# Three placements in the second layer of a two-layer network: convolution pieces, a pair of scalings, and the silu of the third u

## The chip, the cores and the metric

The kernel runs on one core of a Trainium2 chip. The metric is the device time of one execution in microseconds (us), the median of several runs. A profile is one further execution, recorded instruction by instruction. Its engines are PE (matrix multiply; PEld is its weight load), DVE (vector), ACT (scalar, activation functions), POOL (GpSimd) and SP, which here only issues DMAs.

## The reference

The input x has shape 4 x 192 x 128 x 128 in float32. Layer 1 adds a block of fractional and ordinary Fourier transforms; nothing in it is touched here. Layer 2 adds a selective state-space block to x, along the 16384 pixels of an image taken as one sequence:

```python
seq = (seq - mu) * lax.rsqrt(var + LN_EPS) * ln_g + ln_b
xz = jnp.einsum('blc,ec->ble', seq, in_proj_w)
xs, z = jnp.split(xz, 2, axis=-1)
# xc: a causal convolution of 4 taps over xs, channel by channel, + conv_b
u = jax.nn.silu(xc).transpose(0, 2, 1)
x_dbl = jnp.einsum('bld,kd->blk', u, x_proj_w)
dt, Bm, Cm = jnp.split(x_dbl, [DT_RANK, DT_RANK + D_STATE], axis=-1)
dt = jax.nn.softplus(jnp.einsum('blr,dr->bld', dt, dt_proj_w) + dt_proj_b)
A = -jnp.exp(A_log)
def step(hcar, inp):
    dt_t, B_t, C_t, u_t = inp
    dA = jnp.exp(dt_t[..., None] * A)
    hnew = hcar * dA + (dt_t * u_t)[..., None] * B_t[:, None, :]
    y_t = jnp.sum(hnew * C_t[:, None, :], axis=-1)
    return (hnew, y_t)
...
y = ys.transpose(1, 0, 2) + u * Dp
y = y * jax.nn.silu(z)
out = jnp.einsum('bld,cd->blc', y, out_proj_w)
```

There are 384 inner channels and 16 states for each.

## The kernel before

The sequence of each image is cut into 32 chunks of T = 512 pixels, 128 chunks for the four images. The 384 channels are NJ = 3 groups of 128 (one per partition). A chunk is worked in 24 *steps*, k = 0 to 23: group j = k // 8 and pair of states sg = k % 8. A step holds two *scans*, one for each state of the pair. Scan k.0 and scan k.5 are the first and the second of step k.

What a step does, engine by engine:

- DVE runs the two scans (L869), h = h * da + db. The factor `da` = exp(dt * A) comes from ACT (L799). For most scans it lies in a tile `da`, prepared four scans ahead, and the other operand is a PSUM tile `op`.
- The second operand is made in one of three ways. In the steps where sg is 3 or 6 (`BY_PE`), ACT scales blocks of the transposed dt*u by B (`scale_pair`, L843, tile `dbT`, from a transposed copy `tu` that PE writes at L833), and PE transposes them back (`turned_back`, L855, into `op`). In the steps 1, 4, 7, 9, 15, 17 and 23 (`BY_POOL`) POOL multiplies (L827, tile `db`), two steps ahead. There the factor of the scan stands in a PSUM `op`, made by ACT three scans ahead (`decay_there`). In all others DVE multiplies (L819), from dp, an ACT copy of dt*u in PSUM (L782).
- POOL multiplies the two states with C (L882, `hc` <- `h`). The tile h has three buffers, hc five.
- PE sums hc into y by transposing it (L895), three steps later.

Next to these steps runs the *front* of a later chunk, a Python generator, `front(i)`: normalisation, projections, convolution, the making of u, z, dt and B, C. It begins at step 14 of the chunk two before its own, runs through all of the chunk before its own, and each plain `yield` ends its part in one step. `yield MID` puts the next part between the two scans of the same step, `yield LATE` behind both scans. The order of the instructions on each engine is the order in which the Python code emits them (`manual_schedule`). In a step, the emission goes: tails of an earlier chunk, the first `turned_back`, sums, `turned`, the fronts' first parts, POOL's db for the step after next, then the first scan; after it the second `turned_back`, the MID parts and the scalings (`between`); then the second scan, POOL's hc, and the LATE parts.

The front's parts that matter here, with their steps in the chunk before its own: projections of xs (`in_proj`, L666) in step 23 of the chunk before that and in steps 0 and 1 and their copies by ACT (L679) in 0, 1 and 2; the convolution on PE, four taps for each group, in halves (`conv`, L684): c0 in steps 2 and 3, c1 in 4 and 6, c2 in 9 and 10; silu of the first two u in step 8 (L692); projection of z0 in step 12; silu of the third u and of z0 (L692, L696) at the head of step 13; the projection of B, C and dt (px, L728) in step 14.

The front of the chunk after that is at its normalisation in steps 14 to 22: sums on PE (L619, step 15), the centring on DVE (L622, step 16), the variance (L635, step 18), the root on ACT (`rs`, L642, behind step 19's scans), its reciprocal on DVE (L645) and the transpose on PE (L647) behind step 20's scans, the copy `rows` on ACT (L651) and its spreading on PE (L655) in step 21, and the multiplication on DVE (L660) between the scans of step 22.

`TURNED` and `SCALED` say in which steps PE turns a group and ACT scales its pairs. Each group's y is copied by ACT (L904), transposed by PE (L919) and gated by DVE (L924) once a chunk, in the next group's steps. PSUM for the fronts' and tails' products and for `tu` is one pool of three buffers (`ps`). SP issues the DMAs of the carried states and of B and C.

Of the kernel before, what the change touches and what calls it, by code (L numbers as in the profile page):

```python
# [503 lines left out]
def layer1(tc, xmid, out, st2, w, n_tok=S * S):  # L504
# [10 lines left out]
    MID, LATE = "mid", "late"  # L515

    TURNED = {0: 0, 9: 1, 15: 2, 19: 2}
    SCALED = {0: (0, 3), 3: (0, 6), 9: (1, 3), 11: (1, 6), 16: (2, 3), 19: (2, 6)}
    with ExitStack() as ctx:
        def pool(name, bufs, **kw):  # L520
            return ctx.enter_context(tc.tile_pool(name=name, bufs=bufs, **kw))
# [66 lines left out]
        def psum():  # L588
            return ps1.tile([128, 512], F32, name="ps")
# [14 lines left out]
        def front(i):  # L604
# [58 lines left out]
            def in_proj(m):  # L663
                pp = psum()
                for t in range(2):
                    nc.tensor.matmul(  # L666
                        pp, wiT[:, t, m * 128 : (m + 1) * 128], s[:, t, :], start=t == 0, stop=t == 1
                    )
                return pp
# [6 lines left out]
            for j in range(NJ):  # L676
                pp = in_proj(j)
                yield
                nc.scalar.activation(xs[:, j, 3:], pp, AF.Identity, bias=bxz[:, j : j + 1])  # L679
            nc.scalar.copy(halo, xs[:, :, T : T + 3])  # L680

            def conv(j, pc, half):
                for k in (2 * half, 2 * half + 1):
                    nc.tensor.matmul(  # L684
                        pc, dcw[:, j, k, :], xs[:, j, k : k + T], start=k == 0, stop=k == 3
                    )
# [3 lines left out]
            def silu_u(j, pc):  # L690
                u[j] = jp.tile([128, T], F32, name="u")
                nc.scalar.activation(u[j], pc, AF.Silu, bias=cb[:, j : j + 1])  # L692

            def silu_z(j, pp):
                zs[j] = jp.tile([128, T], F32, name="zs")
                nc.scalar.activation(zs[j], pp, AF.Silu, bias=bxz[:, NJ + j : NJ + j + 1])  # L696
# [18 lines left out]
            c2 = psum()  # L715
            conv(2, c2, 0)
            yield
            conv(2, c2, 1)
            yield
            yield  # L720
            z0 = in_proj(NJ)
            yield
            silu_u(2, c2)
            silu_z(0, z0)
            yield
            px = psum()
            for j in range(NJ):
# [109 lines left out]
        def scale_pair(n, j, sg):  # L837

            g = got[n]
            for st in range(sg * G, (sg + 1) * G):  # L840
                t = g["dbT", j, st] = scp.tile([128, T // 128, 128], F32, name="dbT", bufs=2)
                for blk in range(T // 128):
                    nc.scalar.activation(  # L843
                        t[:, blk, :], g["tu", j][:, blk, :], AF.Identity,
                        scale=g["bT"][:, blk, st : st + 1],
                    )
# [102 lines left out]
        def start_front(n):  # L949
            if n < total:  # L950
                fronts.append(front(n))
# [10 lines left out]
        def go_on(parts, part):  # L962

            for f in parts[part]:
                got_on = next(f, None)
                if got_on is not None:
                    parts[got_on].append(f)

        with tc.manual_schedule():
            for i in range(min(2, total)):  # L970
                load_x(i)
            for _ in front(0):
                pass
# [18 lines left out]
            for pos, (n, k) in enumerate(order):  # L992
# [26 lines left out]
                def between():  # L1019
                    go_on(parts, MID)  # L1020
                    if k in SCALED and k:
                        scale_pair(n, *SCALED[k])

# [4 lines left out]
                if k == 0:  # L1028
                    scale_pair(n, *SCALED[k])
                if pos >= LAG and sg == LAG:  # L1030
# [130 lines left out]
def program(tc, x, out, w):  # L1161
    B = x.shape[0]
    with (
        tc.tile_pool(name="keep", bufs=1) as keep,
        tc.tile_pool(name="mid", bufs=1, space=DRAM) as mid,
    ):
        st2 = keep.tile([CH, B, 2, 2], F32, name="st2")
        xmid = [mid.tile([C, S * S], F32, name=f"xmid{b}") for b in range(B)]
        layer0(tc, x, xmid, st2, w)
        layer1(tc, xmid, [out[b].rearrange("c h w -> c (h w)") for b in range(B)], st2, w)  # L1170
# [16 lines left out]
```

## Time and profile before

| | |
|---|---|
| time, median of 3 runs (lowest, highest) | 11583.59 us (11582.08, 11585.74) |
| the profiled execution: its time | 11592.76 us |
| the profiled execution: its span | 11590.8 us |
| mean granted TensorE clock | 0.934 |
| between 2500 and 11000 us (layer 2): POOL, DVE, PE, ACT busy | 8225.6, 8158.0, 8056.5, 7596.2 of 8500 us |
| scan (L869), one | 1267 ns |
| hc on POOL (L882), one | 2366 ns |

The span runs from the first to the last recorded instruction; layer 1 takes about the first 1500 us. In the lists a line gives the source line, the engine, the operation and the tiles as out<-in. In the timeline the first two numbers are the start and the length in us, and the brackets at the end hold the idle time of the engine before it and what ended it. In the list of waits a line says who waited for whom: us in total, times, longest. "issue" stands where the profile shows no releaser.

### The profile page before, as it was taken

The page shows a single profiled execution, that of the slowest core. Times are in us where ns is not written, and L with a number is a line of the kernel's source. Part 1 is how long each engine was busy: PE and PEld are TensorE (multiplying, and loading weights), DVE is VectorE, ACT ScalarE, POOL GpSimd, SP SyncE. Part 2 cuts the span into 40 slices and gives each one's busy share as a digit, 9 for nine tenths or more (in the row PEclk, how much of TensorE's full clock was granted, in tenths as well). Part 3 has the DMA queues.
Part 4 walks back from the last instruction along what each step waited for, and adds up shares of the span by engine and source line. Part 5 has one row for each costly group of instructions (what it writes and reads, how often), then busy time and mean ns, then how long its engine had stood idle before and what let it go on. Part 6 is the DMA issues. An engine that isn't in the chain of part 4 may idle for free.

```text
span 11590.8 us, 163663 instructions
## 1 busy us (share of the span) xinstructions
PE 10615.0 (92%) x54154; PEld 7007.7 (60%) x54154; DVE 10503.1 (91%) x11072; ACT 9334.7 (81%) x17508; POOL 9823.7 (85%) x4470
## 2 busy tenths in 40 slices
PE   4777889999999999999999999999999999999998
PEld 2444356666666666666666666666666666666665
DVE  5565679999999999999999999999999999999999
ACT  2322178988988988988898898898898889889887
POOL 0000069999999999999999999999999999999999
PEclk8878789999999999999999999999999999999999
DMA  8787734434434434433433443443443443444343
GB/s 206 204 218 203 195 102 126 114 115 126 121 108 127 127 103 126 126 108 121 126 113 116 126 120 109 127 126 103 127 126 107 122 126 112 117 126 118 111 126 98
DMA packets 1339433, 1494.73 MB, mean 129 GB/s; under 512 B 903474, under 2 KB 954359, under 8 KB 1338071
## 3 DMA queue, kind: packets, MB, share of 16 engines
q1 hardware_dynamic: 1318102, 1421.34, 42.8%
q0 software_dynamic: 13312, 50.34, 1.3%
q10 hardware_dynamic: 7168, 12.59, 0.3%
q8 instruction: 428, 7.01, 0.3%
q14 instruction: 423, 3.46, 0.1%
HBM read 1325.19 MB, written 155.32 MB: 128 GB/s over the span
## 4 chain that ended last, share of the span: by engine, by line
PE 35%; DVE 28%; ACT 23%; issue 11%; DMA 2%; POOL 1%; DVEq 0%; SPq 0%; ACTq 0%; POOLq 0%
DVE h L869 18%; PE ps L666 8%; ACT da L799 7%; PE py L895 7%; PE ps L684 6%; DVE op L819 5%; PE ps L933 3%; ACT dbT L843 3%; ACT L799 3%; PE op L855 3%; ACT op L799 2%; PE pr L471 2%; ACT s L612 2%; ACT L692 1%; ACT L642 1%
## 5 line engine op out<-in xcount | busy, mean ns | idle before, releaser
L882 POOL TENSOR_TENSOR hc<-h,bc 128x1024 f32<-128x1024 f32 x3072 | 7195.0, 2366 | 342.6 <-DVE h L869 338.2
L869 DVE TENSOR_TENSOR_SCAN h<-da,carry,op 128x512 f32<-128x512 f32 x4216 | 5227.0, 1267 | 115.2 <-PE op L855 110.9
L895 PEld LDWEIGHTS py<-ident,hc 128*128 128x128 f32 x24576 | 2963.8, 147 | 787.8 <-issue 716.3
L895 PE MATMUL py<-ident,hc 128*128 128x128 f32 x24576 | 3360.5, 283 | 25.7 <-POOL hc L882 12.4
L799 ACT ACTIVATE da<-dt,c_A_log 128x512 f32<-128x512 f32 x4352 | 3008.5, 728 | 356.9 <-DVE h L869 349.4
L869 DVE TENSOR_TENSOR_SCAN h<-op,carry,db 128x512 f32<-128x512 f32 x1736 | 2203.2, 1269 | 116.7 <-issue 83.6
L827 POOL TENSOR_TENSOR db<-dtu,bc 128x1024 f32<-128x1024 f32 x896 | 2146.2, 2395 | 6.4 <-DMA bc<-dbc 6.4
L819 DVE TENSOR_TENSOR op<-dp,bc 128x512 f32<-128x512 f32 x2816 | 1897.8, 674 | 32.1 <-ACT dp L782 32.1
L843 ACT ACTIVATE dbT<-ps,bT 128x128 f32<-128x128 f32 x6144 | 1656.8, 379 | 11.8 <-PE ps L833 11.6
L799 ACT ACTIVATE op<-dt,c_A_log 128x512 f32<-128x512 f32 x1792 | 1222.3, 683 | 548.0 <-DVE h L869 546.5
L666 PE MATMUL ps<-s,c_wiT 96*128 96x512 f32 x3072 | 1602.6, 648 | 2.6 <-DVE s L660 2.6
L684 PE MATMUL ps<-xs,dcw 128*128 128x512 f32 x3072 | 1448.4, 594 | 4.2 <-ACT xs L679 1.8
L855 PE MATMUL op<-ident,dbT 128*128 128x128 f32 x6144 | 1084.1, 297 | 102.2 <-DVE h L869 78.3
L855 PEld LDWEIGHTS op<-ident,dbT 128*128 128x128 f32 x6144 | 795.1, 152 | 528.5 <-ACT dbT L843 149.1
L799 ACT ACT_TABLE_LOAD x636 | 816.0, 1283 | 11.2
L666 PEld LDWEIGHTS ps<-s,c_wiT 96*128 96x128 f32 x3072 | 556.7, 201 | 420.4 <-issue 417.1
L933 PE MATMUL ps<-yg,c_woT 128*96 128x512 f32 x1536 | 710.4, 598 | 57.0 <-DVE xm L939 57.0
L684 PEld LDWEIGHTS ps<-xs,dcw 128*128 128x128 f32 x3072 | 523.4, 190 | 380.4 <-issue 371.6
L477 POOL DMA_DIRECT2D xmid<-xt x64 | 42.6, 666 | 792.3 <-DVE xt L475 792.3
L742 PE MATMUL ps<-xd,c_dtT 12*128 12x512 f32 x768 | 443.6, 662 | 99.4 <-ACT dbT L843 76.0
L751 POOL TENSOR_TENSOR dtu<-dt,u 128x512 f32<-128x512 f32 x384 | 477.8, 1272 | 29.5 <-ACT dt L747 29.5
L933 PEld LDWEIGHTS ps<-yg,c_woT 128*96 128x96 f32 x1536 | 239.8, 163 | 423.7 <-issue 307.7
(172 smaller groups left out, 10399.8 us busy)
## 6 DMA issues: line engine op xcount, KB each, us to landing
bc<-dbc SPq DMA_DIRECT2D x1024, 1024.0 KB, 5.8
xt<-in_x SPq DMA_DIRECT2D x192, 768.0 KB, 9.2
xmid<-xt POOLq DMA_DIRECT2D x64, 768.0 KB, 7.1
xm<-xmid SPq DMA_DIRECT2D x128, 384.0 KB, 3.8
carry<-h SPq DMA_DIRECT2D x3072, 1.0 KB, 1.9
out<-xm SPq DMA_DIRECT2D x128, 384.0 KB, 3.3
d<-x ACTq DMA_DIRECT2D x64, 192.0 KB, 8.2
df<-u SPq DMA_DIRECT2D x16, 512.0 KB, 5.0
```

The costliest lines, as they stand in the source:

```text
L666: nc.tensor.matmul(pp, wiT[:, t, m * 128 : (m + 1) * 128], s[:, t, :], start=t == 0, stop=t == 1)
L684: nc.tensor.matmul(pc, dcw[:, j, k, :], xs[:, j, k : k + T], start=k == 0, stop=k == 3)
L751: nc.gpsimd.tensor_tensor(dtu[j], dt[j], u[j], ALU.mult)
L799: nc.scalar.activation(da, got[n]["dt"][j], AF.Exp, scale=A[:, j, st : st + 1])
L819: nc.vector.tensor_tensor(dbs[s], g["dp"], g["bc", k % NG][:, 0, q, :], ALU.mult)
L827: nc.gpsimd.tensor_tensor(db, _bc(g["dtu"][j], 1, G), g["bc", sg][:, 0], ALU.mult)
L843: nc.scalar.activation(t[:, blk, :], g["tu", j][:, blk, :], AF.Identity, scale=g["bT"][:, blk, st : st + 1],)
L855: nc.tensor.transpose(db[:, blk * 128 : (blk + 1) * 128], t[:, blk, :], ident)
L869: nc.vector.tensor_tensor_scan(h[:, q, :], das.pop(s), dbs.pop(s) if db is None else db[:, q, :], 0.0 if ch == 0 else g["before"][:, j, st ...
L882: nc.gpsimd.tensor_tensor(hc, h, g["bc", sg][:, 1], ALU.mult)
L895: nc.tensor.matmul(py[:, blk, :], hc[:, q, blk * 128 : (blk + 1) * 128], ident, start=first, stop=sg == NG - 1 and q == G - 1 and blk == T ...
L933: nc.tensor.matmul(po[0:CH], woT[:, j, t * CH : (t + 1) * CH], g["yg", j], start=j == 0, stop=j == NJ - 1,)
```

## The change

Nothing is added or taken out; five placements differ. The line numbers after the second hunk are larger by 1 to 3 in the changed file.

```diff
@@
-    SCALED = {0: (0, 3), 3: (0, 6), 9: (1, 3), 11: (1, 6), 16: (2, 3), 19: (2, 6)}
+    SCALED = {0: (0, 3), 3: (0, 6), 9: (1, 3), 11: (1, 6), 16: (2, 3), 20: (2, 6)}
@@
                 yield
                 nc.scalar.activation(xs[:, j, 3:], pp, AF.Identity, bias=bxz[:, j : j + 1])
             nc.scalar.copy(halo, xs[:, :, T : T + 3])
+            yield LATE
 
             def conv(j, pc, half):
@@
             c2 = psum()
             conv(2, c2, 0)
             yield
+            yield LATE
             conv(2, c2, 1)
             yield
-            yield
             z0 = in_proj(NJ)
             yield
+            yield MID
             silu_u(2, c2)
             silu_z(0, z0)
+            yield
             yield
             px = psum()
```

In steps: the first half of c0 moves from the head of step 2 to behind its scans, and so on PE from before to behind the second `turned_back` of that step. The second half of c2 moves in the same way in step 10. The projection of z0 moves from the head of step 12 to the head of step 11. The silu of the third u and of z0 move from the head of step 13 to between the scans of step 12. The scalings of pair (2, 6) move from between the scans of step 19, ahead of the root, to between those of step 20, behind it. All that follows (px and on) stays in its step.

## What was predicted

> **What bounds the kernel now.** I read the page, then the waits and busy times of one long stretch of layer 2, then the timelines of POOL, DVE, ACT and PE through one chunk.
>
> ```profile
> PE 10615.0 (92%) x54154; PEld 7007.7 (60%) x54154; DVE 10503.1 (91%) x11072; ACT 9334.7 (81%) x17508; POOL 9823.7 (85%) x4470
> ...
> POOL hc L882 <- DVE h L869: 271.2, 428, 1.4
> ...
> DVE rs L645 <- ACT rs L642: 120.2, 108, 2.1
> ...
> DVE h L869 <- PE op L855: 95.3, 181, 1.3
> ...
> DVE h L869 <- issue: 74.7, 109, 1.0
> ```
>
> The first line is the page's busy line, the others are the waits between 2500 and 11000 us. There layer 2 runs at 78.50 us a chunk (first scan to first scan), so the stretch holds 108.3 chunks. In its 8500 us the windows view gives POOL 8225.6 busy and DVE 8158.0: both nearly full, with 2.53 and 3.16 us idle a chunk. No edit shortens work of either, so the most there is to win is POOL's idle time, 2.53 x 127 chunks = 321 us. I number steps 0 to 23 in a chunk, two scans each (k.0, k.5). POOL's timeline through one chunk (first scan at 6241.6 us) shows where it is idle:
>
> ```profile
> 6266.26 2.41 POOL L827 TENSOR_TENSOR db<-dtu,bc 128x1024 f32<-128x1024 f32 x1
> 6268.62 9.32 POOL L882 TENSOR_TENSOR hc<-h,bc 128x1024 f32<-128x1024 f32 x4
> 6278.69 2.38 POOL L882 TENSOR_TENSOR hc<-h,bc 128x1024 f32<-128x1024 f32 x1 [0.75 <-DVE h L869]
> 6282.26 2.37 POOL L882 TENSOR_TENSOR hc<-h,bc 128x1024 f32<-128x1024 f32 x1 [1.19 <-DVE h L869]
> ...
> 6298.87 2.35 POOL L882 TENSOR_TENSOR hc<-h,bc 128x1024 f32<-128x1024 f32 x1 [0.30 <-DVE h L869]
> ...
> 6316.76 2.35 POOL L882 TENSOR_TENSOR hc<-h,bc 128x1024 f32<-128x1024 f32 x1 [0.20 <-DVE h L869]
> ```
>
> Four waits, each for DVE: hc of steps 11, 12, 17 and 22. By place over 108 chunks they average 0.69, 1.20, 0.30 and 0.34. From hc(22) on POOL has no gap until hc(11) of the next chunk. DVE's own stalls in the same chunk:
>
> ```profile
> 6251.95 1.28 DVE L869 TENSOR_TENSOR_SCAN h<-da,carry,op 128x512 f32<-128x512 f32 x1 [0.84 <-PE op L855]
> ...
> 6268.71 1.28 DVE L869 TENSOR_TENSOR_SCAN h<-op,carry,db 128x512 f32<-128x512 f32 x1 [0.16 <-POOL db L827]
> ...
> 6277.27 1.28 DVE L869 TENSOR_TENSOR_SCAN h<-da,carry,op 128x512 f32<-128x512 f32 x1 [0.21 <-PE op L855]
> ...
> 6288.64 1.28 DVE L869 TENSOR_TENSOR_SCAN h<-op,carry,db 128x512 f32<-128x512 f32 x1 [0.67 <-issue]
> ...
> 6309.69 0.18 DVE L645 RECIPROCAL rs<-rs 128x4 f32<-128x4 f32 x1 [0.98 <-ACT rs L642]
> ...
> 6314.18 1.22 DVE L660 TENSOR_TENSOR s<-s,ps 96x1024 f32<-96x1024 f32 x1 [0.16 <-PE ps L655]
> ```
>
> These are scans 3.5, 9.0, 11.5, 15.0, the reciprocal at the end of step 20, and the multiply inside step 22 (means 0.73, 0.21, 0.17, 0.69, 1.10, 0.17). The two lists make one ring. From hc(22) to db(9) POOL leads: scan 9.0 waits for db(9) in every chunk, so a DVE stall before it (3.5) costs nothing. From 9.0 to 12.5 DVE leads, and POOL's waits at 11 and 12 are the other face of that run. From hc(12) to hc(22) POOL leads again, but for the late scans at 17 and 22.
>
> ACT tells why 15.0 is late; "issue" names nothing, but the scan begins 0.09 after the first op below is done (6287.88 + 0.67 = 6288.55):
>
> ```profile
> 6282.12 0.72 ACT L799 ACTIVATE da<-dt,c_A_log 128x512 f32<-128x512 f32 x1 [1.05 <-DVE h L869]
> 6282.77 0.59 ACT L782 COPY dp<-dtu 128x512 f32<-128x512 f32 x1
> 6283.37 1.28 ACT L692 ACT_TABLE_LOAD   x1
> ...
> 6287.88 0.67 ACT L799 ACTIVATE op<-dt,c_A_log 128x512 f32<-128x512 f32 x1
> ```
>
> ACT idles 0.47 + 1.05 us before two da, then two table loads and two silu hold up everything, and it does not idle again until 6316.6.
>
> [...] op(3.5) stands behind 1.72 us of convolution (6249.53 to 6251.25). [...] The trace has the 1.28, but silu follows 0.02 later, so I take 1.28 alone. In the changed program's order the scalings after the root bring no load, and all 1311 loads of the program remain. [...]
>
> **The change part by part** (times of this chunk; no instruction is added or removed, DVE's, POOL's and SP's orders stay).
>
> 1. *First convolution pieces behind op(3.5)*, step 2. op(3.5) comes up to 1.72 us earlier, which covers the 0.73. DVE reaches 7.0 and 9.0 that much earlier and waits there for db(7) and db(9). Worth 0. Displaced: conv, then py; hc has five buffers and no row shows POOL waiting for PE here.
>
> 2. *Second half of c2 behind op(11.5)*, step 10. Without the 1.72, op(11.5) can be done near 6275.6; scan 11.5 wants it at 6277.06. DVE leads here: -0.17.
>
> 3. *z0's projection a step earlier, silu in the middle of step 12.* PE: conv until about 6277.3, z0 until 6279.1; silu's first load can start at 6279.88, when ACT has finished the two da before. The 3.88 us block (6283.37 to 6287.25) then fills the 1.52 idle. Queued behind it: da(14.0), ready at 6279.88 + 3.88 + 0.72 = 6284.48; scan 14.0 wants it at 6285.52 - 0.21 = 6285.31, a margin of 0.83. Then da(14.5), dp, da(16.0), and op(15.0) ready about 6287.0, wanted at 6287.75 when scan 14.5 ends. So 15.0's 0.69 goes, and DVE is 0.17 + 0.69 = 0.86 earlier at step 17, POOL by 0.17: hc(17) no longer waits: -0.30. ACT does not keep its 1.55: op(17.5) needs the slot that scan 16.0 frees, and before it started 0.04 after that scan's end (6293.46, 6293.50), so ACT runs 0.86 earlier from there on.
>
> 4. *Pair (2,6) scaled behind the root*, step 20. Eight scalings take 2.00 us (6304.60 to 6306.60), so the root is done at 6309.66 - 2.00 - 0.86 = 6306.8; DVE wants it near 6307.9. The 1.10 at the reciprocal vanishes. Next is late: rows (L651), behind the same ACT work as before (2.00 only changed place), so it moves by 0.86 alone: 6312.73 to 6311.87. PE's L655 and the multiply inside step 22 follow; their wait grows from 0.17 to about 1.2. DVE is 0.86 earlier at 22.5, POOL by 0.47: hc(22)'s wait of 0.34 goes, with 0.05 left over. New waits: the pair's scalings (ready about 6308.9, wanted as op(22.0) at 6310.9), and the transpose of rs, whose PSUM buffer is now the one these scalings read: ready at 6308.9, PE comes to it behind the yt transposes at about 6309. If this cover were gone, op(22.0) and rows would be late by what the scalings are, and past 0.05 us it would cost part of the 0.34.
>
> Sum: -0.17 - 0.30 - 0.34 = -0.81 a chunk, times 127 = -102 us. POOL's waits at 11 and 12 stay, at 1.72 together. Against the profiled execution (span 11590.8, its time 11592.76) that is 11490.5; the median shown is 9.2 lower, 11583.6, so the forecast is 11482.
>
> Bounds of what before does not show: part 3's margin of 0.83 may prove too small (a loss below), or POOL may gain less than 0.81 if ACT's lead fades before rows. At most all idle but 11 and 12 goes, 0.17 + 0.64, which is the forecast itself; small shifts in semaphore lag (0.09 a hand-over, some two in the DVE-led run) give 0.2 x 127 = 25 us either way.
>
> **Rivals.**
> - *Only part of it* (18%): the lead at rows is 0.47 or less, since a da or op waits for a DVE event that I took as free. hc(22) keeps its wait: 0.47 x 127 = 60, 11524. For: one gate had 0.04 of margin. Against: the others I followed have 0.3 or more.
> - *Every DVE stall counts* (5%): 0.73 + 0.17 + 0.69 + 1.10 = 2.69, capped by POOL's 2.53, times 127 = 321: 11262. For: DVE is the busier-looking engine of the waits view, and POOL's 271 all name it. Against: scan 9.0 waits for POOL in all chunks, so what DVE gains before it ends there.
> - *No change* (6%): op(15.0) is not what 15.0 waits for, and the root's 2.00 is paid back at rows: only 0.17 x 127 = 22, 11562.
> - *Slower* (6%): the silu block delays da(14.0). It decides from 0.83 + 0.86 = 1.7 us of delay (silu of z would begin at 6281.8, so z0 would have to end 4.4 us after its 6279.1); below that POOL at hc(17) is no later than before. At 2.5 us of delay, 0.8 a chunk: 11583.6 + 102 = 11686. PE without a gap here speaks for it; ACT getting to z 2.7 us after z0 is done against.
>
> **How the numbers follow.** The walk as a whole: 65%, 11482, by itself 11457 to 11507. The part case adds its 11524 with as much above, so the range is 11450 to 11535; it leaves out no change, slower and most of the third rival. Below 0.2% (23 us) this kernel can't be told from no change. Faster: 65 + 18 + 5 = 88%; same 6%; slower 6%.
>
> **What would show it.** Right: no wait at 3.5, 11.5, 15.0 and the reciprocal; about 1 us at 7.0 and 9.0 for POOL, and about 1.2 at L660 for PE; POOL with two waits a chunk, 77.7 us a chunk. Wrong: POOL still waiting at hc(17) or hc(22), or DVE waiting for da at 14.0.

## The result, and the profile after

| | before | after |
|---|---|---|
| time, median of 4 runs (lowest, highest) | 11583.12 us (11582.08, 11585.74) | 11453.55 us (11448.41, 11459.74) |
| profiled execution: time, span | 11592.76, 11590.8 us | 11449.58, 11447.4 us |
| first to last scan of layer 2 | 10044.9 us | 9915.1 us |
| period of a chunk in layer 2 | 78.50 us | 77.49 us |
| mean granted TensorE clock | 0.934 | 0.931 |

The changed kernel takes 0.9888 of the time of before, 95% interval 0.9871 to 0.9905: 129.6 us less. Layer 2 accounts for it: from its first to its last scan it takes 129.8 us less, 1.01 us a chunk. (Between the two profiled executions layer 1 differs by another 13.6 us; nothing in it was edited, and the medians don't show that.)

The busy line of the page, after:

```profile
PE 10543.1 (92%) x54154; PEld 7050.4 (62%) x54154; DVE 10489.8 (92%) x11072; ACT 9324.7 (81%) x17508; POOL 9806.5 (86%) x4470
```

POOL and DVE lost 17 and 13 us of busy time against a span shorter by 143: it was idle time that went. The waits of the changed kernel between 2500 and 11000 us (total, times, longest):

```profile
POOL hc L885 <- PE ps L922: 125.3, 105, 1.2
...
DVE s L660 <- PE ps L655: 122.0, 110, 1.2
...
DVE h L872 <- POOL db L830: 101.6, 292, 0.7
...
POOL hc L885 <- DVE h L872: 50.5, 113, 1.2
...
DVE h L872 <- ACT da L802: 7.9, 25, 0.5
```

DVE no longer waits for `op` or for the root; it waits for POOL (`db`), at the multiply of step 22 for PE, and a little for `da` at scan 22.0. The first line is to be read with care. It is the wait of hc(12), and the releaser named is not what ends it. In POOL's timeline of the chunk that begins at 6165.9 us:

```profile
6192.94 9.34 POOL L885 TENSOR_TENSOR hc<-h,bc 128x1024 f32<-128x1024 f32 x4
6202.72 2.38 POOL L885 TENSOR_TENSOR hc<-h,bc 128x1024 f32<-128x1024 f32 x1 [0.44 <-DVE h L872]
6206.29 2.36 POOL L885 TENSOR_TENSOR hc<-h,bc 128x1024 f32<-128x1024 f32 x1 [1.19 <-PE ps L922]
...
6217.94 6.98 POOL L885 TENSOR_TENSOR hc<-h,bc 128x1024 f32<-128x1024 f32 x3
...
6237.85 4.87 POOL L885 TENSOR_TENSOR hc<-h,bc 128x1024 f32<-128x1024 f32 x2
```

hc(12) starts at 6206.29, and scan 12.5, whose output it reads, ends at 6206.11: POOL waits for DVE there as before (over 107 chunks hc(12) starts 0.17 us after that scan's end, in both kernels). The lines with x3 and x2 hold hc(17) and hc(22), now without a gap before them. DVE in the same chunk (scans 4.0, 7.0, 9.0, the reciprocal, scan 22.0, the multiply):

```profile
6176.73 1.28 DVE L872 TENSOR_TENSOR_SCAN h<-op,carry,db 128x512 f32<-128x512 f32 x1 [0.17 <-POOL db L830]
...
6186.07 1.28 DVE L872 TENSOR_TENSOR_SCAN h<-op,carry,db 128x512 f32<-128x512 f32 x1 [0.40 <-POOL db L830]
...
6193.05 1.28 DVE L872 TENSOR_TENSOR_SCAN h<-op,carry,db 128x512 f32<-128x512 f32 x1 [0.39 <-POOL db L830]
...
6232.02 0.17 DVE L645 RECIPROCAL rs<-rs 128x4 f32<-128x4 f32 x1
...
6235.40 1.28 DVE L872 TENSOR_TENSOR_SCAN h<-da,carry,op 128x512 f32<-128x512 f32 x1 [0.28 <-ACT da L802]
...
6237.79 1.22 DVE L660 TENSOR_TENSOR s<-s,ps 96x1024 f32<-96x1024 f32 x1 [1.12 <-PE ps L655]
```

And ACT around the silu, whose two loads stood behind 0.47 + 1.05 us of idle time before and now follow the da without a gap:

```profile
6202.84 1.39 ACT L802 ACTIVATE da<-dt,c_A_log 128x512 f32<-128x512 f32 x2
6204.24 1.28 ACT L693 ACT_TABLE_LOAD   x1
...
6206.82 1.28 ACT L802 ACT_TABLE_LOAD   x1
...
6210.49 0.67 ACT L802 ACTIVATE op<-dt,c_A_log 128x512 f32<-128x512 f32 x1
```

The op of scan 15.0 is done at 6211.16 and DVE starts that scan at 6211.93 without a wait. By place, in us a chunk over 108 chunks:

| idle time | before | after |
|---|---|---|
| DVE at 3.5, 4.0, 7.0, 9.0 | 0.73, 0, 0.06, 0.21 | 0, 0.19, 0.38, 0.38 |
| DVE at 11.5, 15.0, reciprocal | 0.17, 0.69, 1.10 | 0, 0, 0 |
| DVE at 22.0 and the multiply (L660) | 0, 0.17 | 0.13, 1.11 |
| POOL at hc(11), hc(12), hc(17), hc(22) | 0.69, 1.20, 0.30, 0.34 | 0.42, 1.19, 0, 0.03 |

### The profile page after: what moved, and what is told of

The parts are those of the page before. It is cut to its first block, busy times and chain, and to the rows that moved or that the text cites. A ratio compares the mean times of both kernels' runs of the same rounds, so it can differ in the third digit from the quotient of the medians.

```text
span 11447.4 us, 163662 instructions
## 1 busy us (share of the span) xinstructions
PE 10543.1 (92%) x54154; PEld 7050.4 (62%) x54154; DVE 10489.8 (92%) x11072; ACT 9324.7 (81%) x17508; POOL 9806.5 (86%) x4470
## 4 chain that ended last, share of the span: by engine, by line
ACT 29%; DVE 29%; PE 26%; issue 10%; POOL 3%; DMA 2%; DVEq 0%; ACTq 0%; POOLq 0%; SPq 0%
DVE h L872 21%; ACT da L802 9%; ACT dbT L846 6%; DVE op L822 6%; PE py L898 5%; PE ps L666 4%; PE ps L936 4%; PE ps L685 4%; ACT L802 3%; PE op L858 2%; POOL db L830 2%; ACT op L802 2%; PE pr L471 2%; ACT L693 1%; PE ps L655 1%
## 5 line engine op out<-in xcount | busy, mean ns | idle before, releaser
L898 PEld LDWEIGHTS py<-ident,hc 128*128 128x128 f32 x24576 | 3001.5, 148 | 849.3 <-issue 685.1
L898 PE MATMUL py<-ident,hc 128*128 128x128 f32 x24576 | 3404.1, 285 | 29.9 <-ACT yt L907 17.5
L666 PE MATMUL ps<-s,c_wiT 96*128 96x512 f32 x3072 | 1520.9, 619 | 2.6 <-DVE s L660 2.6
L685 PE MATMUL ps<-xs,dcw 128*128 128x512 f32 x3072 | 1424.3, 592 | 1.5 <-ACT u L693 1.3
L745 PE MATMUL ps<-xd,c_dtT 12*128 12x512 f32 x768 | 514.1, 761 | 164.5 <-DVE s L622 99.7
```

The lines of the kernel that those rows point to most:

```text
L666: nc.tensor.matmul(pp, wiT[:, t, m * 128 : (m + 1) * 128], s[:, t, :], start=t == 0, stop=t == 1)
L685: nc.tensor.matmul(pc, dcw[:, j, k, :], xs[:, j, k : k + T], start=k == 0, stop=k == 3)
L745: nc.tensor.matmul(d[j], dtT[rows, :], xd[rows, :], start=True, stop=True)
L898: nc.tensor.matmul(py[:, blk, :], hc[:, q, blk * 128 : (blk + 1) * 128], ident, start=first, stop=sg == NG - 1 and q == G - 1 and blk == T ...
```

## The experiments

### Each part alone

Four kernels, each the kernel before with one part of the change as the prediction numbers them, and a fifth with two. The cuts below are taken against the changed kernel; the line above each says which of the five have it. (The expectations call PE TensorE, ACT ScalarE and POOL GpSimd.)

```diff
@@ parts 1, 2 and 3 alone, and 2 with 3: no scalings behind the root
-    SCALED = {0: (0, 3), 3: (0, 6), 9: (1, 3), 11: (1, 6), 16: (2, 3), 20: (2, 6)}
+    SCALED = {0: (0, 3), 3: (0, 6), 9: (1, 3), 11: (1, 6), 16: (2, 3), 19: (2, 6)}
@@ all but part 1 alone: c0 in front of the scans
             nc.scalar.copy(halo, xs[:, :, T : T + 3])
-            yield LATE
@@ parts 1, 3 and 4 alone: c2's second half in front of the scans
             yield
-            yield LATE
             conv(2, c2, 1)
             yield
@@ parts 1, 2 and 4 alone: z0 and the silu where they were
+            yield
             z0 = in_proj(NJ)
             yield
-            yield MID
             silu_u(2, c2)
             silu_z(0, z0)
-            yield
             yield
```

Part 1 alone, the first half of c0:

> The kernel before with part 1 alone (first half of c0 behind op(3.5)). Ring theory (a DVE stall counts only in the run from scan 9.0 to 12.5, or where POOL's hc(17) or hc(22) waits): the 0.73 at scan 3.5 goes and comes back as waits for POOL at 4.0, 7.0 and 9.0; 78.50 us a chunk as before, 11583 within 10. Every-stall theory (each DVE stall removed shortens the chunk by its size): 0.73 x 127 = 93 less, 11490.

Measured: 11584.61 us, ratio 1.0 (0.9992 to 1.0009). Nothing, as the forecast has it; but each of the other parts alone measures as nothing too, so this run by itself does not tell why. The wait at 11.5 went too (0.17 to 0.00), and of the 0.18 us that the run from 9.0 to 12.5 lost with it nothing was left at hc(22), where POOL's wait rose from 0.34 to 0.52.

Part 2 alone, the second half of c2:

> The kernel before with part 2 alone (second half of c2 behind op(11.5)). Ring theory: the run from 9.0 to 12.5 is shorter by the wait of 0.17 alone, 22 less, 11561; with the overlap of two neighbouring DVE instructions that a wait destroys (about 0.08, in 85 of 100 chunks) by 0.24, 31 less, 11552. If POOL leads here after all: 11583.

Measured: 11581.83 us, ratio 0.9998 (0.9989 to 1.0007). A miss. The gain came and was given back: POOL's wait at hc(11) fell from 0.69 to 0.41, and its wait at hc(22) rose from 0.34 to 0.63.

Part 3 alone, z0 and the silu:

> The kernel before with part 3 alone (z0 a step earlier, silu in the middle of step 12). Ring theory: the 0.69 at 15.0 goes and nothing later eats it, as ACT's rows come 0.69 earlier too; hc(17) and hc(22) both stop waiting although the reciprocal still waits about 1.1; 0.30 + 0.34 = 0.63 a chunk, 80 less, 11503, up to 11490 with overlaps regained on POOL. Two-keys theory (hc(22) needs the root's move as well): 0.30 to 0.35 a chunk, 38 to 44 less, about 11542. Every-stall theory: 0.69 a chunk, 11496, with DVE waiting at 9.0 no more than before.

Measured: 11583.06 us, ratio 0.9997 (0.9989 to 1.0006). A miss for all that had been expected. The wait at hc(17) went from 0.30 to 0, and that at hc(22) rose from 0.34 to 0.68.

Part 4 alone, the scalings behind the root:

> The kernel before with part 4 alone (pair (2,6) scaled in step 20, behind the root). Ring theory: the wait of 1.10 at the reciprocal goes and the wait at the multiply inside step 22 grows from 0.17 to about 1.2, as rows keeps its place on ACT; hc(22) waits as before; 11583 within 10. Every-stall theory: 1.10 x 127 = 140 less, 11443. Two-keys theory: hc(22)'s 0.34 goes, 43 less, 11540.

Measured: 11585.16 us, ratio 0.9999 (0.999 to 1.0007). The time is as expected, and the wait left the reciprocal and came back at the multiply of step 22 (1.11 us). That hc(22) would wait as before was not so: 0.34 became 0.54.

Parts 2 and 3 together:

> The changed kernel without parts 1 and 4 (that is, before with parts 2 and 3). Ring theory: the same as the changed kernel, 77.49 us a chunk and 11454 within 10, with the stalls at 3.5 and at the reciprocal back at full size. Two-keys theory: hc(22) waits again, 0.34 x 127 = 43 more, about 11497. Every-stall theory: 0.73 + 1.10 a chunk more, no gain left.

Measured: 11571.85 us, ratio 0.999 (0.9984 to 0.9997): 11 us, where 130 had been expected. So part 4, which alone gives nothing, must carry something that the forecast didn't see.

### Is the ring right?

Two kernels add two spare DVE products of 0.42 us (their output is used by nothing) to the changed kernel, once in step 3, where POOL should lead, once in step 11, where DVE should:

```diff
+        spare = cp.tile([128, 256], F32, name="spare")
...
                     go_on(parts, MID)
+                    if k == 3:
+                        for q in range(2):
+                            at = slice(256 * q, 256 * q + 256)
+                            nc.vector.tensor_tensor(spare, got[n]["dp"][:, at], got[n]["bc", sg][:, 0, 0, at], ALU.mult)
```

> The changed kernel with two spare products of 128x256 on DVE (about 0.66 us together, result unused) in the middle of step 3. Ring theory: POOL leads there, DVE's waits at 4.0, 7.0 and 9.0 (0.19 + 0.38 + 0.38 = 0.95 a chunk) take them up; 11454 within 10. Every-stall theory: 0.66 x 127 = 84 more, 11538.

Measured: 11460.54 us, 7.0 above the changed kernel (ratio to before 0.9892, 0.9875 to 0.9908). In step 11 (`k == 11`):

> The changed kernel with the same two spare products in the middle of step 11, inside the run from 9.0 to 12.5. Ring theory: the chunk is longer by all of them, POOL's waits at 11 and 12 grow by about 0.66; 84 more, 11538. If POOL leads everywhere: 11454.

Measured: 11574.07 us, 120.5 above the changed kernel (ratio to before 0.9992, 0.9983 to 1.0001). The two products take 0.84 us, not the 0.66 expected. The same work cost 0.06 us a chunk before scan 9.0, and 0.92 behind it. In step 11 the run from 9.0 to 12.5 is longer by 0.79 us, and POOL's wait at hc(11) by as much (0.42 to 1.21); the other 0.13 us come from something else, which the next part finds. The ring stands. A third kernel takes work off the DVE-led run: of the two output sums of a chunk (L942, 0.66 us each) the second goes to PE as one more product with the identity, and ACT copies it.

```diff
+                if t:
+                    nc.tensor.matmul(
+                        po[0:CH], ident[0:CH, 0:CH], xm[:, t, :], start=False, stop=True
+                    )
...
+                if t:
+                    nc.scalar.copy(xm[:, t, :], po[0:CH])
+                else:
+                    nc.vector.tensor_add(xm[:, t, :], po[0:CH], xm[:, t, :])
```

> The changed kernel with the second addition of the output (DVE, L942 in the middle of step 10, inside the run from 9.0 to 12.5) made on PE, as one more matrix product of identity and xm into the same sum, and copied out by ACT. Ring theory: the run is shorter by the 0.58 from that addition's start to the next scan's, POOL's waits at 11 and 12 shrink from 1.6 to about 1.0; 0.58 x 127 = 74 less than 11454, 11380. If POOL's waits there are not set by this run: no gain, 11454; if ACT's added 0.57 us delays da(14.0) or PE's added product delays op(11.0), 11454 or more.

Measured: 11392.87 us (11387.91 to 11398.98), ratio to before 0.9834 (0.982 to 0.9849). It is faster than both kernels, by 60.7 us against the changed one, and POOL's wait at hc(11) is gone: 76.99 us a chunk, with POOL idle for 1.11. The run is shorter by 0.59 us, as expected; 0.09 of it is lost again in the rest of the ring, so the gain is 0.50 a chunk.

### Where a single part's gain goes

The ring, cut at four events of every chunk, shows it. The run from scan 9.0 to the end of scan 12.5 is DVE's; what follows it up to `rows` (L651) is ACT's; from hc(22) to scan 9.0 POOL leads, with 30.32 to 30.37 us in all these kernels. Means over 107 chunks, us; the third and fourth columns are taken from the end of scan 12.5:

| kernel | run 9.0 to 12.5 | ACT's square (L627) | rows | ACT's wait for PE between the two | period |
|---|---|---|---|---|---|
| before | 13.33 | 15.27 | 30.77 | 0.10 | 78.50 |
| part 1 | 13.14 | 15.27 | 30.97 | 0.26 | 78.51 |
| part 2 | 13.06 | 15.27 | 31.08 | 0.35 | 78.50 |
| part 3 | 13.36 | 14.47 | 30.78 | 0.81 | 78.51 |
| part 4 | 13.16 | 15.27 | 30.98 | 0.20 | 78.51 |
| parts 2, 3 | 13.06 | 14.47 | 30.94 | 0.99 | 78.41 |
| changed | 13.06 | 14.48 | 29.97 | 0.06 | 77.49 |

Take the wait from `rows` minus the square, and 15.4 to 15.5 us are left in every row: behind the square ACT has a fixed amount of work, and the one thing that varies is its wait for PE. Part 3 brings the square 0.80 us forward, and 0.71 us more of waiting takes it back. What ACT waits for are PE's transposes of dt*u (`tu`; the expectations below say "of u"), which the scalings of pair (2, 6) read. (With the scalings behind the root, in the rows part 4 and changed, it is the transpose for `bT`, which stands on PE just behind.) In ACT's timeline of the kernel with part 3 alone (chunk from 6225.0 us):

```profile
6286.74 0.56 ACT L905 COPY yt<-py 128x512 f32<-128x512 f32 x1
6288.04 0.89 ACT L844 ACTIVATE dbT<-ps,bT 128x128 f32<-128x128 f32 x3 [0.74 <-PE ps L834]
```

PE in the same stretch:

```profile
6275.30 1.12 PE L743 MATMUL ps<-xd,c_dtT 12*128 12x512 f32 x2
6277.24 1.12 PE L743 MATMUL ps<-xd,c_dtT 12*128 12x512 f32 x2 [0.82 <-DVE s L622]
6278.94 2.07 PE L743 MATMUL ps<-xd,c_dtT 12*128 12x512 f32 x2 [0.58 <-ACT dbT L844]
6280.94 1.97 PE L896 MATMUL py<-ident,hc 128*128 128x128 f32 x8
6282.70 1.06 PE L856 MATMUL op<-ident,dbT 128*128 128x128 f32 x4
...
6287.31 0.64 PE L834 MATMUL ps<-ident,dtu 128*128 128x128 f32 x4
```

PE works without a gap from 6278.94 to the transposes. But the third dt product takes 2.07 us where the first two took 1.12, and the sums into y take 1.97 where eight such take 1.04 at full clock. The windows view of that stretch says why. Its stretches of 3.41 us are bounded by the grid of the trace's clock records (PE busy comes first behind the length, and the granted clock is the third number from the end):

```profile
6274.81:6278.23 3.42, 2.60 (x10) 0.91 (x7) 3.42 (x4) 2.45 (x8) 3.42 (x3) 1.00 0.12 19
6278.23:6281.64 3.41, 2.83 (x7) 1.20 (x7) 3.41 (x5) 3.39 (x7) 3.41 (x2) 0.50 0.04 0
6281.64:6285.05 3.41, 3.41 (x18) 3.41 (x18) 3.41 (x4) 3.38 (x5) 3.41 (x3) 0.50 0.04 0
6285.05:6288.46 3.41, 3.41 (x33) 3.41 (x33) 3.41 (x5) 2.65 (x6) 3.41 (x4) 1.00 0.06 5
```

In the traces of before and of the changed kernel 0.5 and 1.0 are the only values granted, and all clock records (566 and 460) begin on one grid of 3413.3 ns, within 1 ns, over the whole execution. A stretch between two lines of this grid is called a window here. Of the 218 halved stretches of before behind 2500 us 215 are one or two windows long, of the 175 of the changed kernel 173. In the four above, the window with the hole of 0.82 us (PE busy for 2.60 of 3.42) is followed by a halved one, that one holds the hole of 0.58 (2.83 of 3.41) and is followed by another, and after a full window the clock is whole again.

PE's busy share in a window does not by itself settle what is granted in the next: in the last kernel shown below a window with 3.17 us busy is followed by a halved one, and one with 3.12 is not. What settles it stays open.

This also bears on the equal periods of before and of the four single parts, 78.50 to 78.51 us: 23 windows of 3413.3 ns are 78.507, and in the trace of before the mean period of 107 chunks is 78.507 too. These kernels keep their place on the windows ("held" below). The table shows where a chunk's first scan stands, as against a clock that ticks every 23 windows and is set to 0 at chunk 13 (us, minus is early; chunks are numbered 0 to 127, and 32, 64 and 96 begin a new image):

| kernel | chunk 31 | 36 | 50 | 63 | 68 | 82 | 95 | 114 |
|---|---|---|---|---|---|---|---|---|
| before | -0.7 | -0.6 | -0.6 | -0.7 | -0.3 | -0.4 | -0.4 | -0.3 |
| part 3 | -0.1 | -0.6 | -0.1 | -0.1 | -0.6 | -0.1 | -0.1 | -0.1 |
| part 4 | 0.0 | -0.4 | 0.0 | 0.0 | -0.4 | 0.0 | 0.0 | 0.0 |
| parts 2, 3 | -0.1 | -3.3 | -3.6 | -3.6 | -6.7 | -7.0 | -7.0 | -10.4 |
| changed, spare work in step 11 | -0.5 | -2.0 | -3.5 | -3.6 | -5.0 | -6.8 | -7.3 | -10.2 |
| changed | -17.8 | -23.5 | -37.4 | -50.5 | -56.0 | -70.1 | -83.2 | -102.6 |

Single chunks of before and of the four parts alone take 77.6 to 79.3 us, yet in 107 chunks none of these five kernels strays over more than 1.3 us. The kernel with parts 2 and 3 is held as well. At each new image it loses some 2.3 us at once; the next chunks take 78.2, 78.2, 78.3 and 78.4 us, and about ten chunks later it rests again, one window (3.4 us) earlier, at 78.51 us a chunk. Its 78.41 instead of 78.51, and so nearly all of the 11 us that parts 2 and 3 gained, are these jumps. The changed kernel with the spare work in step 11 does likewise, only more slowly, and its 78.41 lies above 77.49 + 0.84 = 78.33. The changed kernel itself (22.70 windows a chunk) moves on by a window every three to four chunks and is not held.

### Two tests of this

If part 4 helps because, behind the root, its scalings ask for `tu` later, then parts 3 and 4 together must give most of the gain. The kernel is the changed one without parts 1 and 2. (The expectation says step 14; the silu is in step 12, as in the change.)

> Silu of the third u in step 14 and the pair's scalings behind the root (parts 3 and 4), without the two convolution halves (parts 1 and 2). Theory of ScalarE and TensorE (the ring runs from scan 12.5 over ScalarE's work to the row sums, and ScalarE's way to the root is held by TensorE's transposes of u in step 19): each part alone gave nothing because the other's hold was left, so together they give nearly all: from the end of scan 12.5 to the row sums near 30.0 us instead of 30.8, chunk period 77.5 to 77.75, total 11455 to 11490. Rival (the parts add up as they did alone): 11583, within 5. Rival (the second convolution half is what makes the others pay): 11560 or more.

Measured: 11479.9 us (11477.05 to 11484.87), ratio 0.9909 (0.9894 to 0.9924). ACT's wait for the transposes is gone (0.06 us, for another product), `rows` comes at 29.98 and the period is 77.66. Two parts that give nothing each give 105.7 us together. With part 2 as well, without part 1:

> The changed kernel without part 1 (the convolution's first half of c0 back in front of the scan of step 3.5). Both theories: the wait at 3.5 comes back (near 0.7 us) and is worth nothing, since GpSimd leads there: 11454, within 10. Rival (all parts are needed together): 11520 or more.

Measured: 11456.35 us, ratio 0.9888 (0.9874 to 0.9903): another 23.6 us, the run 9.0 to 12.5 at 13.06 instead of 13.23. The wait at 3.5 is back (0.46) and costs nothing: 2.8 us above the changed kernel, within what single runs differ by. Over 127 chunks these 2.8 us put its period, by estimate, at 0.02 above the changed kernel's 77.49, so it is not held at 78.51, and this is the run that shows part 1 to be worth 0.

The second test leaves the scalings ahead of the root and mends the clock instead. To the kernel with part 3 alone it adds spare products of u, seven of about 0.9 us by estimate (three real ones take 2.84 in before's timeline, at 6285.66), ahead of the dt products; the real ones overwrite what they write.

```diff
             for j in range(NJ):
+                for _ in range((4, 3, 0)[j]):
+                    nc.tensor.matmul(d[j], xpT[:, j, :], u[j], start=True, stop=True)
                 rows = slice(32 * j, 32 * j + RANK)
```

> The silu's move alone (part 3), with seven spare TensorE products of u ahead of the two real dt products in step 16, written where the real ones then overwrite them. Theory that the halved clock in steps 17 to 19 is what delays the transposes of u: halved-clock time per chunk falls from 9.8 us to under 6, the transposes end at least 1 us earlier after scan 12.5 (21.9 us in the silu-only kernel), ScalarE's 0.81 us wait for them goes, period near 77.7, total near 11490. Rival (not the clock but TensorE's own queue of work, or the period is set elsewhere): halved-clock time may fall, the total stays at 11583 or is above it by the spare work, up to 11680.

Measured: 11657.0 us, ratio 1.0062 (1.0045 to 1.0079). A miss. Halved-clock time fell from 9.8 us a chunk to 1.5, but the transposes began later still, at 22.5 us after scan 12.5 instead of 21.9 (where the expectations let them "end" or be "done", the figure is that of their start): by estimate 6.4 us of products in holes of 1.4 us put PE's own queue in the way, and ACT now waited for dt (0.69) too. It doesn't tell what the clock alone does. Hence the same with as much as fits the holes:

```diff
-                for _ in range((4, 3, 0)[j]):
+                for _ in range((1, 1, 0)[j]):
```

> The silu's move alone (part 3), with one spare TensorE product of u ahead of the first and one ahead of the second dt product of step 16 (0.9 us each), written where the real ones then overwrite them: as long as the two holes of 0.8 and 0.6 us that TensorE has there in the silu-only kernel, where the seven of the run before were far longer than the holes. Clock theory (the holes bring on the halved clock of steps 17 to 19, and it delays the transposes of u): halved-clock time per chunk under 6 us instead of 9.8, transposes done by 21.5 us after scan 12.5 instead of 21.9, ScalarE's 0.81 us wait for them under 0.3 us, period 77.6 to 78.1, total 11480 to 11540. Rival (the clock is not what holds them, or the period is set elsewhere): transposes at 21.9 us or later, total 11583 or up to 20 more.

Measured: 11514.91 us (11512.58 to 11517.86), ratio 0.994 (0.9923 to 0.9956). As the clock theory expected. Two useless products a chunk make the kernel with part 3 alone 68 us faster. PE in the same stretch (chunk from 6196.9 us):

```profile
6246.96 1.02 PE L743 MATMUL ps<-u,c_xpT 128*128 128x512 f32 x2
6247.92 1.12 PE L745 MATMUL ps<-xd,c_dtT 12*128 12x512 f32 x2
6248.99 1.12 PE L743 MATMUL ps<-u,c_xpT 128*128 128x512 f32 x2
6250.05 1.77 PE L745 MATMUL ps<-xd,c_dtT 12*128 12x512 f32 x4
6251.75 1.10 PE L898 MATMUL py<-ident,hc 128*128 128x128 f32 x8
...
6257.10 0.63 PE L836 MATMUL ps<-ident,dtu 128*128 128x128 f32 x4
```

and its windows, on the grid of the clock records again:

```profile
6250.87:6254.28 3.41, 3.12 (x22) 2.13 (x22) 3.41 (x5) 3.38 (x5) 3.41 (x3) 1.00 0.04 0
6254.28:6257.69 3.41, 3.17 (x30) 2.93 (x29) 3.41 (x4) 3.38 (x5) 3.41 (x3) 1.00 0.09 1
6257.69:6261.11 3.42, 2.72 (x14) 2.35 (x13) 3.42 (x5) 3.42 (x12) 3.42 (x3) 0.50 0.09 9
```

The two spare products lie in the two holes, PE has no gap from 6246.96 to 6252.85, and the clock stays at 1.00 until the transposes are all but done. They begin 60.2 us after the chunk's start instead of 62.3. On average they begin at 20.21 us after scan 12.5 instead of 21.89, halved-clock time is 5.25 us a chunk, ACT's wait for them 0.07, and `rows` comes at 29.95, as early as in the changed kernel. The rest is lost behind it: the way from `rows` to the multiply takes 1.90 us instead of 1.45 and lies in the halved stretch that now comes later (last line). The period is 78.03 on average, and POOL waits 0.39 at hc(22).

## Why the prediction was right

The forecast of 11482 was 28 us above the measured 11453.55, within its range and just outside the likeliest case's own. The markers came as written: nothing at 3.5, 11.5, 15.0 and the reciprocal, 1.11 us at the multiply (written: about 1.2), 0.75 at 7.0 and 9.0 (about 1), 77.49 us a chunk (77.7), POOL with its two waits at 11 and 12. None of the rivals came about.

**Part 1, worth 0.** Right: taken out of the changed kernel it leaves 11456.35. That it gives nothing alone (11584.61) is no proof, since alone every part gave nothing.

**Part 2, −0.17.** Right in the whole (23.6 us in the last step from two parts to three, 0.19 a chunk), and worth nothing alone.

**Parts 3 and 4, −0.30 and −0.34.** The sum is right, the split is not. "ACT runs 0.86 earlier from there on" holds for the change as a whole (the square 0.79 earlier, `rows` 0.80), but not for part 3 by itself. There the forecast walked from the silu over op(17.5) to `rows` without asking which engine could hold ACT on the way: PE's transposes of step 19 did, and there was no slack: ACT waited for them already in the kernel before, 0.10 us a chunk. Of part 4 it saw that the 2.00 us of scalings only change their place for `rows`, which is why it gives nothing alone. It missed that the scalings behind the root also ask later for what PE makes: 0.75 us of ACT's waiting (0.81 with part 3 alone, 0.06 with both). So the walk to `rows` left out a hold that by itself takes all of the 0.64 (part 3 alone: 11583.06). That another part of the same change lifts it was luck, not forecast. Nor did the forecast see the windows of the clock, on which the kernel before and each part alone stay, at 78.50 to 78.51 us a chunk, but not the changed one (77.49).

**The size.** The sum was −0.81 a chunk (times 127 that is 103, not 102), measured −1.01. The terms, from the four cuts of the ring:

| term | forecast | measured |
|---|---|---|
| run 9.0 to 12.5 | −0.17 | 13.33 to 13.06: −0.27 |
| end of 12.5 to hc(22) | −0.64 | 34.81 to 34.11: −0.70 |
| hc(22) to scan 9.0 | 0 | 30.37 to 30.32: −0.05 |

The forecast took for a wait what the profile records as idle. But two DVE instructions without a wait between them overlap: in before's timeline (6247.50) a line of three scans lasts 3.61 us, three single ones of 1.267 last 3.80, so some 0.09 a pair. A wait that goes returns its idle time and this overlap: 0.17 + 0.09 is the 0.27 within the rounding. By estimate the input must come well ahead for that: in parts 1 and 4 alone the wait at 11.5 is gone too, but the run is shorter by 0.18 and 0.16 only. On POOL four hc in a row take 9.32 us and 4 x 2.366 is 9.46, so 0.05 a pair; two waits gone and 0.03 left of them give 0.61 + 0.10, the measured 0.70. The last row's 0.05 is not explained. The forecast's cap ("at most all idle but 11 and 12 goes") fell for the same reason, and since the shorter DVE run also took 0.27 from the wait at 11.

What is shown: that the ring decides where a stall counts (step 3 against step 11), that parts 3 and 4 pay together only, that the halved clock of PE is what holds part 3 alone (two fillers free it), and that before, the single parts and two more kernels are held at 23 windows a chunk (their first scans return to it after each new image). Not shown is by which steps a chunk comes back to the windows, and what decides that a window is halved.

## What to carry to other kernels

When an engine is moved forward, follow it to every event of another engine that it meets on the way to the next bound, and ask what slack is there. Single parts of a change can each measure as nothing and give 1% together, so test pairs before discarding one. A removed wait can return more than its recorded idle time: its two neighbours overlap then, here by 0.09 us on DVE and 0.05 on POOL.

If the period of a loop doesn't move by a hundredth under different edits, divide it by the length of a window of PE's granted clock (3.413 us in these traces; 78.50 to 78.51 us are 23 of them), and look at that clock along the loop. While the loop is held on the windows, an edit that measures as nothing is not shown to be worth nothing: four parts left it at 78.50 to 78.51 us alone and took 1.01 off together. In this kernel a hole of 0.8 us was followed by a halved window, and two fillers of 1.02 us, or a later consumer, gained more than it cost. Here the filler had to fit the hole: two products gained 68 us, seven lost 74.

## What was not expected of the hardware

- Useless work on PE made a kernel faster: two products of 1.02 us a chunk, 0.5 us a chunk less.
- Before and four edited kernels ran at 78.50 to 78.51 us a chunk, 23 times the 3.413 us of the grid on which PE's clock records begin, although the run 9.0 to 12.5 differed by 0.30 us among them. Two others were thrown off by each new image and came to rest on the windows again within some ten chunks.
- PE's clock is halved for 6.8 us of a chunk in the kernel before and for 7.2 in the changed one, with PE's longest idle time in layer 2 at 1.1 us in the one and 1.3 us in the other.
- The releaser named for POOL's longest wait after the change (125 us, "PE ps L922") is not the one it waits for, and "issue" at scan 15.0 before was ACT's op: both are told by which event ends just before the start.
